# Key and value products of pairs of kv heads by Strassen's method in a fused two-layer transformer kernel

## The chip, the cores and the metric

The kernel runs on one core of one Trainium2 chip. TensorE (PE) multiplies matrices, VectorE (DVE), ScalarE (ACT) and GpSimd (POOL) do elementwise work and reductions, and SyncE (SP) issues nearly all DMA transfers in this kernel. The metric is the device time of one execution in microseconds (us). Its size is judged by the median of several runs.

## The reference

Two layers work on `x` of 4 batches x 512 rows x 512 columns, in float32. Each layer modulates `x` by an adaptive layer norm, adds a gated attention and then a gated feed-forward network (FFN). The change lies in the attention of layer 1 and at the start of the FFN after it. What is computed there:

```python
# h: modulated layer norm of x, (4, 512, 512); Hq, Hkv, D = 32, 8, 128; g = 4
q = (h @ w_q).reshape(B, S, Hkv, g, D)        # w_q 512 x 4096
k = (h @ w_k).reshape(B, S, Hkv, D)           # w_k 512 x 1024
v = (h @ w_v).reshape(B, S, Hkv, D)           # w_v 512 x 1024
scores = einsum('bqhgd,bkhd->bhgqk', q, k) * D ** -0.5
probs = softmax(where(causal, scores, -inf))
x = x + ga * (einsum('bhgqk,bkhd->bqhgd', probs, v).reshape(B, S, Hq * D) @ w_o)
h = layernorm(x) * (1 + cb) + sb
x = x + gb * down_scale * ((silu(gate(h)) * up(h)) @ down_wq.T)   # weights are integers with scales
```

## The kernel before

Layer 0 takes the first 190 us or so, the attention of layer 1 the time up to about 1778 us, and the FFN of layer 1 the rest. The attention is written out by hand, so each engine takes its instructions in the order in which the Python code emits them. The FFN is ordered by a scheduler.

**Blocks and windows.** The attention runs over 32 blocks `n`: 4 batches x 8 kv heads, each kv head with its 4 query heads. A block has two windows, `2n` (called even here) and `2n+1` (odd). A call `window(w, fill)` works on a pair of query heads: it computes scores and softmax of the next pair, heads `2w+2` and `2w+3`, in eight tiles of 128 rows (four for each head, of 512, 384, 256 and 128 columns because of the causal mask), and multiplies the probabilities of the current pair, heads `2w` and `2w+1`, by the values. It goes through slots `i`: in slot `i` it transposes tile `i-2` (`flip`, blocks of 32x32 on VectorE), normalizes tile `i-1` (`divide`, ScalarE), computes tile `i` (`score`: PE, mask and maximum on VectorE, exp on ScalarE), then in slots 6 and 8 runs `value` for one head of the current pair (PE lines `av`), and then takes its share of the list `fill`: pieces of the large products that belong to later or earlier blocks. The list is spread evenly over nine slots.

**The carry.** The transposed 32x32 blocks have to change partitions. `carry(w+1)` at the end of a window issues 16 DMA transfers of 128 KB on SyncE, from one of two buffers `prob2` (named `p` and `x` in the profile, since the second lies in the memory of `x`) to the tile `turned`, which `value` of the next window reads. There is one `turned`, so the carry starts when the last `value` of the window has read it. For the last pair of heads there is no later window: `turn` transposes its tiles on PE (lines `pT`) and ScalarE copies them into `straight`, which lies in the memory of `prob2[0]`.

**The large products.** Query (`q_pieces`) and output (`o_pieces`) products of a block are 512x512x512 and use Strassen's method in Winograd's form: seven products of quarters 256x256x256 instead of eight. A piece is one quarter product: `seven` takes a PSUM bank, issues 2x2 matmuls with 256 moving columns (lines `quarter`), and `take` adds the result to where it belongs. The weights' sums come from GpSimd (`left_sums`, `right_sums`), as do the sums of the attention output (`sums_o`); the sums of `h` are kept in `hsum` for a whole batch. Key and value products are plain: `k_pieces(n)` uses 4 matmuls of 512 columns for one head (lines `kps`), `v_pieces(n)` 16 matmuls of 128 columns (lines `vps`), each evicted by one ScalarE operation. All pieces share the three PSUM banks of `ps_sc`. The even windows take the query pieces of block `n+1` and the value pieces of block `n+1`, the odd ones the output pieces of block `n-1` and the key pieces of block `n+2`.

**Loads.** SyncE issues them in the order of the code: `load("q", n+2)` at the end of the even window and `load("o", n)` at the end of the odd one, both ahead of the carry, since `window` runs the list `late` before it; the key and value weights after the odd window. `load` has one buffer for each kind, so a load waits for the last matmul that reads the old weights.

**Around the FFN.** `small_loads` at block 23 loads scales, and the FFN's gates `gb` of the four batches, which GpSimd multiplies by the down scales. `leave_attention` puts the attention's result into `x`; for the last batch it stands at the start of the FFN, where its gates `ga` come by DMA. `first_weights` and `split_pieces` in the last block prepare the FFN's first weights and its first input, the latter on PE and ScalarE in pieces that fill the window. At the FFN's start `load(1)`, then `load(2)` and so on bring and convert the other weights.

Of the kernel before, what the change touches and what calls it, by code (L numbers as in the profile page):

```python
# [17 lines left out]
P = 128  # L18
# [15 lines left out]
def adaln_two_layers(ctx: ExitStack, tc: tile.TileContext, a, out: bass.AP):  # L34
# [5 lines left out]
    gp = ctx.enter_context(tc.tile_pool(name="gate", bufs=B))  # L40
# [8 lines left out]
    tmpp = early.enter_context(tc.tile_pool(name="tmp", bufs=2))  # L49
# [77 lines left out]
    def add_scaled(b, t, ps, gate):  # L127

        tm = tmpp.tile([P, E], F32, tag="tm", name="tm")
        nc.vector.tensor_tensor(tm, ps, gate, ALU.mult)  # L130
        nc.gpsimd.tensor_tensor(x[b][:, t, :], x[b][:, t, :], tm, ALU.add)

# [12 lines left out]
    l0x = l0.enter_context(tc.tile_pool(name="l0x", bufs=2))  # L145
    manual = tc.manual_schedule()
# [57 lines left out]
    def load(kind, n, place=None):  # L204

        g = n % HKV
        w = T["wp"].tile([P, KC, GW if kind in "qo" else D1], F32, tag=f"w{place or kind}", name=f"w{kind}1")
        if kind == "o":
            src = a["L1_attn_w_o"][g * GW : (g + 1) * GW, :]
        else:  # L210
            c = w.shape[2]
            src = a[f"L1_attn_w_{kind}"][:, g * c : (g + 1) * c]
        nc.sync.dma_start(w, src.rearrange("(k p) n -> p k n", p=P))
        weights[kind, n] = w
# [12 lines left out]
    def quarters(t):  # L227
        lo, hi = slice(0, HALF), slice(HALF, S)
        return t[:, 0:2, lo], t[:, 0:2, hi], t[:, 2:4, lo], t[:, 2:4, hi]
# [24 lines left out]
    def sums_q(n):  # L254
        s = T["wp"].tile([P, 3, 2, HALF], F32, tag="sq", name="sq")
        left["q", n] = left_sums(nc.gpsimd, weights["q", n], s)
# [25 lines left out]
    class Pieces:  # L282
# [52 lines left out]
        def wsq(self):  # L335
            sums_q(0)
# [392 lines left out]
    def seven(A, Bs, take, order):  # L729

        def piece(i):
            ps, l, r = bank([P, 2, HALF], "quarter"), A()[i], Bs()[i]
            for m in range(2):
# [27 lines left out]
    def q_pieces(n):  # L761
        u, c = {}, {}
        tt = nc.vector.tensor_tensor

        def take(i, ps):
            if i == 1:
                for j in range(2):
                    qT[n, j] = at.tile([P, 2, S], F32, tag="qT", name="qT", bufs=3)
                c[11], c[12], c[21], c[22] = corners(qT[n, 0], qT[n, 1])
                u[1] = at.tile([P, 2, HALF], F32, tag="u1", name="u1", bufs=1)  # L770
                nc.scalar.copy(u[1], ps)
            elif i == 6:
                u[2] = at.tile([P, 2, HALF], F32, tag="u2", name="u2", bufs=1)
                tt(u[2], u[1], ps, ADD)
            elif i == 2:
                tt(c[11], u[1], ps, ADD)
            elif i == 5:
                tt(u[1], u[2], ps, ADD)
            elif i == 7:
                tt(c[22], u[1], ps, ADD)  # L780
                tt(u[2], u[2], ps, ADD)
            elif i == 3:
                tt(c[12], u[1], ps, ADD)
            else:
                tt(c[21], u[2], ps, SUB)

        return seven(lambda: left["q", n], lambda: right["h", n // HKV], take, (1, 6, 2, 5, 3, 7, 4))
# [9 lines left out]

    def k_pieces(n):
        hold = {}

        def piece(i):
            if i == 0:
                hold["ps"] = bank([P, 512], "kps")
            for k in (2 * i, 2 * i + 1):
                nc.tensor.matmul(  # L805
                    hold["ps"], weights["k", n][:, k, :], h1[n // HKV][:, k, :],
                    start=(k == 0), stop=(k == KC - 1),
                )
            if i == 1:
                kT[n] = at.tile([P, S], F32, tag="kT", name="kT")  # L810
                nc.scalar.mul(kT[n], hold["ps"], float(D1) ** -0.5)  # L811

        return [lambda i=i: piece(i) for i in range(2)]

    def v_pieces(n):
        hold = {}

        def piece(i):
            if i == 0:
                hold["ps"] = bank([P, 512], "vps")  # L820
            for t in (2 * i, 2 * i + 1):
                for k in range(KC):
                    nc.tensor.matmul(  # L823
                        hold["ps"][:, t * D1 : (t + 1) * D1],
                        h1[n // HKV][:, k, t * P : (t + 1) * P], weights["v", n][:, k, :],
                        start=(k == 0), stop=(k == KC - 1),
                    )
            if i == 1:
                vs[n] = at.tile([P, NT, D1], F32, tag="v", name="v")
                nc.scalar.copy(vs[n].rearrange("p t d -> p (t d)"), hold["ps"])  # L830

        return [lambda i=i: piece(i) for i in range(2)]
# [198 lines left out]
    def small_loads():  # L1031
# [3 lines left out]
        dsb = tmpp.tile([P, E], F32, tag="tm", name="dsb")  # L1035
        nc.sync.dma_start(dsb, a["L1_ffn_down_scale"].partition_broadcast(P))
        for b in range(B):
            gb[b] = spread(1, 1, b, gp, "gb")
# [16 lines left out]
    def split_pieces(got):  # L1055

        def piece(c):
# [7 lines left out]
            tm = tmpp.tile([P, E], F32, tag="tm", name="tm")  # L1065
# [27 lines left out]
    def window(w, fill, side=(), late=()):  # L1093
# [5 lines left out]
        share = [len(fill) // 9 + (i < len(fill) % 9) for i in range(9)]  # L1099
        each = -(-len(side) // 9)  # L1100
        for i in range(10):
            if more and i > 1:
                (turn if w + 1 == LAST else flip)(*tiles[i - 2])
# [4 lines left out]
            if w >= 0 and i in (6, 8):  # L1108
# [299 lines left out]
```

## Time and profile before

| | |
|---|---|
| Median of 3 runs | 2101.63 us (2101.59 to 2102.39) |
| Profiled execution | 2105.77 us, of which its span 2104.0 |
| PE, share of the span | 98% |
| VectorE, ScalarE, GpSimd | 61%, 43%, 31% |
| Matmul rows `quarter`, `sc`, `av` in the chain | 36%, 13%, 13% |
| Matmul rows `vps`, `kps` in the chain | 5%, 5% |

The profiled execution is one run with the profiler on; it took 4.1 us more than the median. Its rows name line, engine, operation and tiles as `out<-in`; in brackets stand the idle time of the engine ahead of a row and what ended it. Busy times of PE rows overlap somewhat[...]. A block takes some 48.4 us in the steady part, from the start of one block's even window to the next.

### The profile page before, as it was taken

The numbers are of one execution on the slowest core, as the hardware profiler recorded it, in microseconds if no ns is written. First come the engines' busy times: TensorE is split into PE (matmuls) and PEld (weight loads), VectorE is DVE, ScalarE is ACT, GpSimd is POOL, SyncE is SP. The second block draws the span as 40 slices with busy tenths as digits, with TensorE's granted clock in tenths as the row PEclk, the third lists the DMA queues.
The fourth block names the chain that finished last, engine by engine and source line by source line (L and its number), as shares of the span: only waits on it lengthen the run. The fifth ranks groups of instructions, "written<-read, shape, count | busy, mean of one in ns | idle before, by whom it ended". The sixth has DMA issues, their size and how long they took to land.

```text
span 2104.0 us, 26905 instructions
## 1 busy us (share of the span) xinstructions
PE 2053.3 (98%) x9155; PEld 1558.1 (74%) x9155; DVE 1291.7 (61%) x3102; ACT 898.0 (43%) x2029; POOL 654.3 (31%) x525
## 2 busy tenths in 40 slices
PE   6999899999999999999999999999999998999998
PEld 4655677777777777777777777777777776788886
DVE  6766656666656666656676666566565665754543
ACT  3421644445444444544444454444444443332221
POOL 3314123333236222343352234335233322510010
PEclk8799999999999999999999999999999999999999
DMA  8311556665556656556665565566556545500000
GB/s 298 114 51 51 165 152 157 155 178 141 151 156 177 181 142 160 160 144 156 176 184 148 147 179 139 141 169 168 140 148 164 146 119 183 161 21 1 21 21 22
DMA packets 260516, 288.55 MB, mean 137 GB/s; under 512 B 23746, under 2 KB 200898, under 8 KB 260372
## 3 DMA queue, kind: packets, MB, share of 16 engines
q1 hardware_dynamic: 259844, 285.71, 50.1%
q8 instruction: 75, 1.23, 0.2%
q10 hardware_dynamic: 528, 1.05, 0.2%
q14 instruction: 69, 0.57, 0.1%
HBM read 142.99 MB, written 11.57 MB: 73 GB/s over the span
## 4 chain that ended last, share of the span: by engine, by line
PE 93%; DVE 2%; SPq 1%; POOL 1%; ACT 1%; DMA 1%; issue 1%; ACTq 0%; POOLq 0%; DVEq 0%
PE quarter L735 36%; PE av L914 13%; PE sc L865 13%; PE vps L823 5%; PE kps L805 5%; PE acc L1287 5%; PE p_gate L1268 4%; PE p_up L1268 4%; PE ffn L625 2%; SPq L905 1%; PE lnT L468 1%; PE modps L381 1%; PE lg L584 1%; PE qkv_ps L498 1%; PE modT_ps L394 1%
## 5 line engine op out<-in xcount | busy, mean ns | idle before, releaser
L865 PE MATMUL sc<-kT,qT 128*128 128x512 f32 (+3 forms) x1024 | 360.0, 434 | 0.7 <-ACT kT L811 0.7
L914 PE MATMUL av<-x,v 128*128 128x512 f32 x1008 | 295.3, 436 | 6.0 <-DMA wv<-in_L_attn_w_v_dram 3.7
L866 DVE TENSOR_TENSOR sc<-sc,mask 128x128 f32<-128x128 f32 x512 | 145.4, 284 | 227.3 <-PE sc L865 227.0
L914 PEld LDWEIGHTS av<-x,v 128*128 128x128 f32 x1008 | 190.2, 192 | 125.4 <-issue 80.6
L868 DVE TENSOR_REDUCE nmx<-sc 128x1 f32<-128x512 f32 (+3 forms) x512 | 251.5, 491 | 17.7
L880 ACT ACTIVATE p<-p,rden 128x512 f32<-128x512 f32 (+3 forms) x256 | 143.8, 562 | 258.9 <-DVE rden L879 258.9
L880 ACT ACTIVATE x<-x,rden 128x512 f32<-128x512 f32 (+3 forms) x256 | 143.8, 562 | 245.3 <-DVE rden L879 245.3
L865 PEld LDWEIGHTS sc<-kT,qT 128*128 128x128 f32 x1024 | 190.4, 191 | 40.0 <-issue 16.3
L794 DVE TENSOR_TENSOR acc<-acc,quarter 128x512 f32<-128x512 f32 x196 | 134.4, 687 | 132.4 <-PE quarter L735 130.5
L735 PEld LDWEIGHTS quarter<-wo,oT 128*128 128x128 f32 x768 | 146.4, 191 | 54.5 <-issue 28.7
L735 PE MATMUL quarter<-wo,oT 128*128 128x256 f32 x768 | 182.4, 381 | 2.4 <-DMA wo<-in_L_attn_w_o_dram 2.2
L235 POOL TENSOR_TENSOR sq<-wq 128x512 f32<-128x512 f32 x32 | 40.6, 1268 | 424.8 <-DMA wq<-in_L_attn_w_q_dram 418.5
L870 ACT ACTIVATE p<-sc,nmx 128x512 f32<-128x512 f32 (+3 forms) x256 | 135.0, 527 | 73.5 <-DVE nmx L868 34.0
L870 ACT ACTIVATE x<-sc,nmx 128x512 f32<-128x512 f32 (+3 forms) x256 | 134.8, 527 | 73.5 <-DMA x<-p 37.0
L235 POOL TENSOR_TENSOR soT<-oT 128x512 f32<-128x512 f32 x31 | 39.4, 1272 | 373.0 <-PE quarter L735 359.0
L883 DVE STREAM_TRANSPOSE p<-p 128x512 f32<-128x512 f32 (+3 forms) x256 | 129.6, 506 | 21.2 <-ACT p L880 19.7
L883 DVE STREAM_TRANSPOSE x<-x 128x512 f32<-128x512 f32 x248 | 125.6, 506 | 14.9 <-ACT x L880 13.1
L823 PE MATMUL vps<-wv,hT 128*128 128x128 f32 x1024 | 124.8, 275 | 0.0
L735 PE MATMUL quarter<-hsum,sq 128*128 128x256 f32 x512 | 121.0, 379 | 1.4 <-DVE hsum L248 1.4
L735 PE MATMUL quarter<-hsum,wq 128*128 128x256 f32 x512 | 121.1, 379 | 0.0
L735 PE MATMUL quarter<-so,soT 128*128 128x256 f32 x512 | 121.1, 379 | 0.0
L735 PE MATMUL quarter<-hT,wq 128*128 128x256 f32 x512 | 120.9, 379 | 0.0
(232 smaller groups left out, 3593.9 us busy)
## 6 DMA issues: line engine op xcount, KB each, us to landing
x<-p SPq DMA_DIRECT2D x512, 128.0 KB, 2.7
x<-x SPq DMA_DIRECT2D x496, 128.0 KB, 2.6
wq<-in_L_attn_w_q_dram SPq DMA_DIRECT2D x32, 1024.0 KB, 5.2
wo<-in_L_attn_w_o_dram SPq DMA_DIRECT2D x32, 1024.0 KB, 5.1
wm<-in_L_wmod_dram SPq DMA_DIRECT2D x12, 1024.0 KB, 9.8
wk<-in_L_attn_w_k_dram SPq DMA_DIRECT2D x32, 256.0 KB, 3.2
wv<-in_L_attn_w_v_dram SPq DMA_DIRECT2D x32, 256.0 KB, 3.5
xn<-x_d SPq DMA_DIRECT2D x28, 256.0 KB, 4.0
```

Of the source, the lines that this page charges most:

```text
L735: nc.tensor.matmul(ps[:, m, :], l[:, k, m * P : (m + 1) * P], r[:, k, :], start=(k == 0), stop=(k == 1),)
L794: nc.vector.tensor_tensor(osum[:, i - 1], osum[:, i - 1], ps, ADD)
L805: nc.tensor.matmul(hold["ps"], weights["k", n][:, k, :], h1[n // HKV][:, k, :], start=(k == 0), stop=(k == KC - 1),)
L823: nc.tensor.matmul(hold["ps"][:, t * D1 : (t + 1) * D1], h1[n // HKV][:, k, t * P : (t + 1) * P], weights["v", n][:, k, :], start=(k == 0) ...
L865: nc.tensor.matmul(ps[:, :w], q[:, i * P : w], kT[n][:, :w], start=True, stop=True)
L866: nc.vector.tensor_tensor(ps[:, i * P : w], ps[:, i * P : w], mask, ADD)
L868: nc.vector.tensor_reduce(nmx, ps[:, :w], AX.X, ALU.max, negate=True)
L870: nc.scalar.activation(blocks(s, i), ps[:, :w].rearrange("p (j q) -> p j q", q=BK), AF.Exp, bias=nmx, accum_out=den,)
L880: nc.scalar.mul(p, p, rden)
L883: nc.vector.transpose(blocks(s, i), blocks(s, i))
L914: nc.tensor.matmul(av.rearrange("p (a n) -> p a n", a=NG)[:, :, BK * k :], vs[n][:, k, :], pT[:, k, :, P * (s % 2) + BK * k : P * (s % 2 + ...
L1268: nc.tensor.matmul(ps[kind], w[kind][:, k, c * P : (c + 1) * P], h2[b % 2][i][:, k, :], start=(k == 0 and i == 0), stop=(k == KC - 1 and i ...
```

## The change

Key and value products are made for a pair of kv heads at once, 512x256x512 and 512x512x256, by the same seven quarter products: `k_pieces(m)` and `v_pieces(m)` for kv heads `2m` and `2m+1`. A key piece is 2 matmuls of 256 moving columns, a value piece 4 of 128. `take` becomes `gather`, shared by query, key and value; for the keys it scales too. Weights are loaded for pairs (512 KB), and GpSimd makes their sums a block ahead (`pending`). Both products now stand in even windows, the keys of the next pair where `n` is odd, the values of the current pair where `n` is even; odd windows hold output pieces alone. The first three windows are filled anew, with `value` at slots 8 and 9. In the last window of the loop `turn` follows `score` five slots later instead of two, the window has twelve slots, and the last output pieces move into it. The FFN's gates are loaded and multiplied at the start of the FFN, in its own pool, and two pools go or shrink.

```diff
 def load(kind, n, place=None):
-        g = n % HKV
-        w = T["wp"].tile([P, KC, GW if kind in "qo" else D1], F32, tag=f"w{place or kind}", name=f"w{kind}1")
+        pair = kind in "kv"
+        g = n % (HKV // 2) if pair else n % HKV
+        c = 2 * D1 if pair else GW
+        w = T["wp"].tile([P, KC, c], F32, tag=f"w{place or kind}", name=f"w{kind}1")
...
-    def sums_q(n):
-        s = T["wp"].tile([P, 3, 2, HALF], F32, tag="sq", name="sq")
-        left["q", n] = left_sums(nc.gpsimd, weights["q", n], s)
+    def sums_in(kind, n):
+        w = weights[kind, n]
+        s = T["wp"].tile([P, 3, 2, w.shape[2] // 2], F32, tag=f"s{kind}", name=f"s{kind}")
+        left[kind, n] = left_sums(nc.gpsimd, w, s)
...
         def piece(i):
-            ps, l, r = bank([P, 2, HALF], "quarter"), A()[i], Bs()[i]
-            for m in range(2):
+            l, r = still()[i], moving()[i]
+            tiles = l.shape[2] // P
+            ps = bank([P, tiles, r.shape[2]], "quarter")
+            for m in range(tiles):
...
+    def gather(start, scale=None):
+        u, c = {}, {}
+        def plus(out, v, ps, sign=1):
+            if scale is None:
+                nc.vector.tensor_tensor(out, v, ps, ADD if sign > 0 else SUB)
+            else:
+                nc.vector.scalar_tensor_tensor(out, ps, sign * scale, v, ALU.mult, ADD)
         def take(i, ps):
             if i == 1:
...
+                if scale is None:
+                    nc.scalar.copy(u[1], ps)
+                else:
+                    nc.scalar.mul(u[1], ps, scale)
             elif i == 6:
+                plus(u[2], u[1], ps)
             elif i == 2:
+                plus(c[11], u[1], ps)
             elif i == 5:
+                plus(u[1], u[2], ps)
             elif i == 7:
+                plus(c[22], u[1], ps)
+                plus(u[2], u[2], ps)
             elif i == 3:
+                plus(c[12], u[1], ps)
             else:
+                plus(c[21], u[2], ps, -1)
...
+    def k_pieces(m):
+        def start():
+            for n in (2 * m, 2 * m + 1):
+                kT[n] = at.tile([P, S], F32, tag="kT", name="kT", bufs=3)
+            return corners(*(kT[n].unsqueeze(1) for n in (2 * m, 2 * m + 1)))
+        return seven(
+            lambda: left["k", m], lambda: right["h", 2 * m // HKV],
+            gather(start, float(D1) ** -0.5), SEVENTH,
+        )
+    def v_pieces(m):
+        def start():
+            for n in (2 * m, 2 * m + 1):
+                vs[n] = at.tile([P, NT, D1], F32, tag="v", name="v")
+            v0, v1 = vs[2 * m], vs[2 * m + 1]
+            return v0[:, :2], v0[:, 2:], v1[:, :2], v1[:, 2:]
+        return seven(lambda: right["h", 2 * m // HKV], lambda: left["v", m], gather(start), SEVENTH)
...
+    def gates(pool):
+        dsb = pool.tile([P, E], F32, name="dsb")
         nc.sync.dma_start(dsb, a["L1_ffn_down_scale"].partition_broadcast(P))
         for b in range(B):
-            gb[b] = spread(1, 1, b, gp, "gb")
+            gb[b] = spread(1, 1, b, pool, f"gb{b}")
             nc.gpsimd.tensor_tensor(gb[b], gb[b], dsb, ALU.mult)
...
-            tm = tmpp.tile([P, E], F32, tag="tm", name="tm")
+            tm = at.tile([P, E], F32, tag=f"u{1 + c % 2}_{E}", name="tm", bufs=1)
...
-    def window(w, fill, side=(), late=()):
+    def window(w, fill, side=(), late=(), values=(6, 8)):
...
-        share = [len(fill) // 9 + (i < len(fill) % 9) for i in range(9)]
+        lag, turn_ = (5, turn) if w + 1 == LAST else (2, flip)
+        slots = lag + 7
+        share = [len(fill) // slots + (i < len(fill) % slots) for i in range(slots)]
...
+    sums_in("k", 0)
+    sums_in("v", 0)
     sums_wo(0)
...
-    window(-1, v_pieces(0) + k_pieces(1) + q[:1])
+    window(-1, v_pieces(0))
...
-        v = v_pieces(n + 1) if ahead else []
-        k = k_pieces(n + 2) if n + 2 < NBLK else []
+        k = k_pieces(n // 2 + 1) if n % 2 and ahead else []
+        v = v_pieces(n // 2) if n % 2 == 0 and n > 0 else []
...
-            window(0, q[1:], (), [lambda: load("q", 2)])
+            window(0, q[:5], values=(8, 9))
         elif ahead:
             late = [lambda: load("q", n + 2)] if n + 2 < NBLK else []
-            window(2 * n, q + v, side[0], late)
+            if n == 1:
+                fill = q
+            elif k:
+                fill = k[:5] + q[:5] + q[5:] + k[5:]
+            else:
+                fill = [f for i in range(3) for f in (v[2 * i], v[2 * i + 1], q[i])] + v[6:] + q[3:]
+            window(2 * n, fill, side[0], late)
         else:
             first_weights()
-            window(2 * n, o[:5] + split_pieces(got))
+            t = split_pieces(got)
+            window(2 * n, o[:2] + t[:2] + o[2:3] + t[2:] + o[3:])
...
-        if n + 2 < NBLK:
-            sums_q(n + 2)
+        if 0 < n < NBLK - 2:
+            sums_in("q", n + 2)
+        while pending:
+            sums_in(*pending.pop())
         if n == 0:
-            window(1, v + k)
+            window(1, q[5:] + k_pieces(1), (), [lambda: load("q", 2)], (8, 9))
+            sums_in("q", 2)
         else:
-            window(2 * n + 1, o + turns_ + k, side[1], [lambda: load("o", n)])
+            window(2 * n + 1, o + turns_, side[1], [lambda: load("o", n)])
         sums_o(n)
-        if n + 3 < NBLK:
-            load("k", n + 3)
-        if n + 2 < NBLK:
-            load("v", n + 2)
+        m = n // 2 + 2 if n else 2
+        if (n % 2 and n > 1 or n == 0) and 2 * m < NBLK:
+            load("k", m)
+            pending.append(("k", m))
+        if n % 2 == 0 and n > 0 and n + 2 < NBLK:
+            load("v", n // 2 + 1)
+            pending.append(("v", n // 2 + 1))
...
             load(1)
+            gates(fx)
```

## The prediction

> **What bounds the kernel now.** I read the shares by engine and the row of slices first, then busy time by stretch, then TensorE in order of time, last the waits and the queue of SyncE.
>
> ```profile
> PE 2053.3 (98%) x9155; PEld 1558.1 (74%) x9155; DVE 1291.7 (61%) x3102; ACT 898.0 (43%) x2029; POOL 654.3 (31%) x525
> ...
> PE   6999899999999999999999999999999998999998
> ...
> PE 93%; DVE 2%; SPq 1%; POOL 1%; ACT 1%; DMA 1%; issue 1%; ACTq 0%; POOLq 0%; DVEq 0%
> ```
>
> TensorE is busy 98% and is 93% of the chain that ended last. Modelled ends can hide small gaps, so I check attention by stretch: an even window, an odd window, and the last odd window, which has no K product.
>
> ```profile
> 994.56:1018.85 24.29, 24.29 (x121) 19.66 (x120) 14.61 (x39) 11.46 (x28) 8.55 (x8) 1.00 0.67 173
> 1018.85:1043.01 24.16, 24.16 (x98) 17.62 (x97) 15.68 (x41) 11.08 (x27) 6.67 (x6) 1.00 0.65 174
> 1700.59:1721.31 20.72, 20.72 (x91) 16.09 (x89) 13.96 (x37) 10.12 (x25) 1.27 (x1) 1.00 0.45 106
> ```
>
> The columns are length, then busy PE, PEld, DVE, ACT, POOL, then clock and DMA. PE fills each stretch, at full clock; the others have a third free. So PE work taken out of a window shortens it, until something else binds. The prices, from PE in order of time:
>
> ```profile
> 1017.07 1.95 PE L823 MATMUL vps<-wv,hT 128*128 128x128 f32 x16
> 1018.85 1.02 PE L865 MATMUL sc<-kT,qT 128*128 128x512 f32 x2
> 1019.72 1.89 PE L735 MATMUL quarter<-wo,oT 128*128 128x256 f32 x8
> 1021.44 0.81 PE L865 MATMUL sc<-kT,qT 128*128 128x384 f32 x2
> ...
> 1037.42 1.88 PE L805 MATMUL kps<-hT,wk 128*128 128x512 f32 x4
> 1039.13 2.32 PE L914 MATMUL av<-x,v 128*128 128x512 f32 x8
> ```
>
> Start to next start is the true price, since the ends overlap. An f32 matmul shows as two rows. One row of 128 columns costs (1018.85-1017.07)/16 = 0.111 us, of 256 columns (1021.44-1019.72)/8 = 0.215, of 512 columns (1039.13-1037.42)/4 = 0.43: the price is columns, with no fixed part to see.
>
> [...] the gating `acc<-acc,ga` takes 1138 ns beside GpSimd where `acc<-acc,quarter` with a PSUM input takes 687. The new VectorE operations have one PSUM input, so more GpSimd work shouldn't slow them. [...]
>
> **The change part by part.**
>
> 1. *K and V products.* K of a pair was 2x4 matmuls of 512 columns: 16 rows x 0.43 = 6.88 us. Now 7 quarters x 2 matmuls x 2 rows = 28 rows of 256 x 0.216 = 6.05: 0.83 less. V was 64 rows of 128 x 0.112 = 7.17; now 7x8 = 56 rows, 6.27: 0.90 less. 16 pairs x 1.73 = **27.7 us less PE work**, all on the path.
>
> Evictions: ACT had 4 of 0.59 us a pair, now 2 of half the width. VectorE gets 14 of 128x256 from PSUM a pair. No such row exists; between 128x128 (284 ns) and 128x512 (687 ns) lies 0.42 us[...]. So 2.9 us for K or for V, each in an even window of its own: 14.6+2.9 = 17.5 of some 26.9 us, hidden beside the quarters on PE. GpSimd gets 8 sums of 128x256 a pair; no such row either, so half to all of the 1.27 us of 128x512: 5 to 10 us a pair of two blocks (95 us), a block ahead of use, with the GpSimd queue idle for most of a block now (418.5 us in all for `wq`): hidden. The weights come as 16+16 loads of 512 KB for 32+32 of 256 KB, the same bytes, on SyncE behind a carry and a block ahead of use: hidden. I cost these at nothing, and likewise the split's `tm` in the tiles of `u1` and `u2`, whose writer, ACT, has ended with them by then.
>
> 2. *Windows become uneven.* K moves out of the odd windows: even ones take 24.3-3.6+6.1 = 26.8 us (V: 27.0), odd ones 24.2-3.4 = 20.7. The odd window needs 15.7 us of VectorE, 76%. The third stretch above is such a window, 20.72 us without a PE gap (without the two `sizes` reductions, 1.4 us). So I take 0 lost; bounds 0 and 0.7 a window.
>
> 3. *The carry.* At a window's end SyncE issues 16 copies of probabilities, which wait until the last `av` has read `turned`; the next `av` waits for all 16.
>
> ```profile
> 1013.13 0.38 SPq L213 DMA_DIRECT2D wq<-in_L_attn_w_q_dram  x1
> 1017.26 10.66 SPq L905 DMA_DIRECT2D x<-x  x16
> ...
> 1067.58 11.78 SPq L905 DMA_DIRECT2D x<-x  x16
> ```
>
> Issue 10.3 to 11.8 plus 2.6 to landing is 12.9 to 14.4 us from the end of `av`. The next `av` comes at slot 6: one piece, 7 score tiles (4.1) and 6 output pieces (10.4), 16.2 us (K: 15.4). Slack 1 to 3. In the even windows with V the fill now ends with the last q quarter, after that `av`, and the load of `wq` for n+2 waits for that quarter. SyncE runs in order, so the carry queued behind it starts 1.73+0.05+0.38 = 2.2 us later, with 1 MB in front of it. It lands at 15.1 to 16.6, plus 0 to 1.6 for the shared engines, against 16.2. 14 windows; 0 to 1 us each; I take **+2 in all**. After odd windows the carry starts 1.1 us late (as it did at 1722.40, `av` having ended at 1721.31), but the next `av` is over 17 us away.
>
> 4. *Start.* PE stood 0.69 for `kT`, 3.73+0.25 and 1.61+0.45 us in windows -1 to 1, the 3.73 being the first carry (landing 239.2). K's two last pieces now cover the first. In window -1 only V is left as fill, so the first carry is set by VectorE: 8 tiles x 1.35 + 7 x 0.42 = 13.7 us plus the tail, from 211 to 227, landing at 240. `av` has been put at slots 8 and 9, about 236: 4 us lost, then about 1: **-1.5** (-4 to +3).
>
> 5. *Last pair.* PE waited 3.09, 0.42, 0.33 and 2.55 us in the turns:
>
> ```profile
> 1736.97 0.55 PE L893 MATMUL pT<-ident,x 128*128 128x128 f32 x3 [3.09 <-ACT x L880]
> ...
> 1751.65 0.44 PE L893 MATMUL pT<-ident,x 128*128 128x128 f32 x2 [2.55 <-ACT x L880]
> ```
>
> ACT stood until 1735.8 because the first turned tile overwrites what the carry still reads, and all later tiles queued behind. With turns three slots later the first comes at about 1733.6, so ACT stands 1.7 us and PE has 5 us of other work that needs no freed bank. 6.4 lost becomes 1: **-5.4** (-6.4 to 0). The remaining waits (2.16 for `wo`, 0.5 for `so`) stay.
>
> 6. *FFN gates.* Five broadcasts (256 KB each) and four GpSimd products leave block 23, where they were hidden, for the FFN's start. SyncE issues them between the first and second weight loads, 5 x 0.5 us; 1.28 MB at the 280 GB/s seen there is 4.6 us, so `ga` for the last batch lands at about 1792 (old time scale) instead of 1785.6, and four gatings stand on VectorE ahead of the third hidden tile, which it reached at 1796.9; GpSimd is 5 us later with the second weights, used at 1802.5. **+1** (0 to 4).
>
> Sum: -27.7+2-1.5-5.4+1 = **-31.6 us**. The profiled execution took 2105.77 us (span 2104.0), 4.1 above the median of 2101.63. I apply the sum to the median: **2070**.
>
> **Rivals.**
> - *The short odd windows bind on VectorE or on banks.* For: 76% mean, and six slots in a row hold score and output work. Against: the 20.72 us stretch. At 0.7 us x 31: 2092.
> - *The new order starves `av`: slower.* If the 1 MB of `wq` lands (5.1 us after issue) before the carry moves, the carry lands at 2.2+5.1+13 = 20.3, 4.1 after PE wants it; 14 x 4.1 = 57: 2127. It decides from (33.6/14) 2.4 us a window. Against: wide loads run at near 400 GB/s, so 1 MB is 2.6 us, and carries issue slower than the engines take them.
> - *The work goes but PE gaps.* A K piece is 0.86 us, and three banks wait for VectorE. If each of 224 pieces leaves 0.13 us, 29 us return: 2099, no change. Against: bursts are two pieces a slot, with 0.4 us each to empty.
>
> **How the numbers follow.** My forecast, 2063 to 2078, has 0.66; better (no mid loss, start at its best) 0.06; the odd windows 0.14; no change 0.05; starved `av` 0.09. Faster 0.86, same 0.05, slower 0.09, where 0.2%, 4.2 us, is about what a measurement of this kernel can tell from no change. The range 2061 to 2092 takes in the forecast, its unknown terms and the first rival.
>
> **What would show it.** Right: no `kps` or `vps` rows, `quarter` rows up by 448 of 256 and 896 of 128 columns at unchanged prices; a pair of blocks at 95.2 us instead of 96.9; `av` not waiting for DMA; turns waiting under 2 us. Wrong: PE gaps before `av` at slot 6 of odd windows after V windows (starved), or before `sc` and `quarter` in odd windows (VectorE); prices above 0.22 and 0.115 us a row.

## The result: 2110 us instead of 2105, slightly slower

In 20 runs each, on the same chips, the changed kernel has a median of 2110.22 us (2101.1 to 2119.62) and the kernel before 2104.86 (2101.59 to 2115.7). The ratio is 1.0025, with a 95% interval of 1.0012 to 1.0037: slower by about a quarter of a per cent, at the edge of what can be measured, and 40 us from the forecast of 2070. Of these, 3.2 us lie in the base: the forecast was put on a median of three runs of the kernel before, 2101.63. The profiled execution of the changed kernel took 2109.82 us (span 2107.9), against 2105.77 before.

The page of the changed kernel: busy time by engine, the shares of the chain that ended last, the group of `av` rows (busy us, mean ns, idle us ahead of them and what ended most of it), and the copies of the carry into the second buffer (KB each, median us from issue to landing).

```profile
PE 2037.2 (97%) x9219; PEld 1582.1 (75%) x9219; DVE 1360.0 (65%) x3326; ACT 873.5 (41%) x1997; POOL 748.6 (36%) x653
...
PE 80%; DMA 7%; SPq 5%; DVE 3%; issue 2%; POOL 2%; ACT 1%; POOLq 0%; ACTq 0%; DVEq 0%
...
L917 PE MATMUL av<-x,v 128*128 128x512 f32 x1008 | 299.6, 441 | 28.9 <-DMA x<-x 13.9
...
x<-x SPq DMA_DIRECT2D x496, 128.0 KB, 2.9
```

PE is busy for 16 us less, yet the span is 4 us longer. (The 16 are less than the 27.7 of work that went. Of the 11.6 between, an estimate from the granted clock in slices of 1 us gives 5 to rows at a lower clock: busy time times the missing clock adds up to 30.2 us, before to 24.9. The rest is not assigned; the last section comes to such rows.) PE's share of the chain has fallen from 93% to 80%, and DMA with SyncE's queue has grown from 2% to 12%. The `av` rows stand idle for 28.9 us; before it was 6.0. By stretch, four windows of blocks 26 and 27 (columns as in the prediction: length, busy PE, PEld, DVE, ACT, POOL, clock, DMA share, GB/s): even with V, odd, even with K, odd.

```profile
1481.84:1508.81 26.97, 26.97 (x146) 22.35 (x145) 16.46 (x47) 12.46 (x32) 8.86 (x7) 1.00 0.49 129
1508.81:1531.40 22.59, 20.96 (x90) 16.01 (x88) 14.82 (x39) 9.57 (x24) 9.23 (x9) 1.00 0.63 150
1531.40:1558.16 26.76, 26.76 (x118) 21.42 (x117) 16.75 (x47) 12.08 (x31) 8.87 (x7) 1.00 0.59 160
1558.16:1578.88 20.72, 20.72 (x89) 16.09 (x88) 14.60 (x39) 9.54 (x24) 9.24 (x9) 1.00 0.50 125
```

Three of the four are what the prediction said, 27.0, 26.8 and 20.7 us. The odd window after V should take 20.7 too: it has 20.96 us of PE work and lasts 22.59. What ends the gap, on PE:

```profile
1504.93 2.32 PE L917 MATMUL av<-x,v 128*128 128x512 f32 x8
1507.09 1.89 PE L733 MATMUL quarter<-hsum,wq 128*128 128x256 f32 x8
1508.81 1.02 PE L868 MATMUL sc<-kT,qT 128*128 128x512 f32 x2
...
1525.06 2.40 PE L917 MATMUL av<-x,v 128*128 128x512 f32 x8 [1.63 <-DMA x<-x]
...
1534.63 1.03 PE L733 MATMUL quarter<-hT,wk 128*128 128x256 f32 x4
1535.49 1.03 PE L733 MATMUL quarter<-hsum,wk 128*128 128x256 f32 x4
```

A key piece starts 0.86 us before the next, as priced. But `av` of the odd window stands for its carry. Thirteen of the 14 odd windows after a V window whose `wq` load stands before the carry have such a wait; against 22.45 us from second `av` to second `av` without one, they lose 0.98 to 3.87 us each, 24.1 us in sum. In the fourteenth, block 22, PE had already stood 1.17 us for `size` on VectorE, as in the kernel before. SyncE and VectorE around the same window end:

```profile
1509.04 0.37 SPq L208 DMA_DIRECT2D wq<-in_L_attn_w_q_dram  x1
1509.95 12.80 SPq L908 DMA_DIRECT2D x<-x  x16
```

```profile
1506.69 0.12 DVE L882 RECIPROCAL rden<-den 128x1 f32<-128x1 f32 x1
1509.01 0.69 DVE L765 TENSOR_TENSOR qT<-u,quarter 128x512 f32<-128x512 f32 x1 [2.20 <-PE quarter L733]
1509.62 0.30 DVE L886 STREAM_TRANSPOSE x<-x 128x128 f32<-128x128 f32 x1
```

The second `av` ends at 1507.09. The first copy of the carry is issued at 1509.95, 2.86 us later, right after the last `flip` (L886). That flip's input was ready, but VectorE stood 2.20 us for the last q quarter, whose eviction (L765) is ahead of it in VectorE's order: the code of slot 8 emits `value` and then the fill piece, slot 9 the flip. The 16 copies then take 12.8 us to issue, with the 1 MB of `wq` issued 0.91 us ahead of them. Meanwhile the DMA engines are busy 97% (226 GB/s); over the carry from 1559.07 to 1569.38, issued 4.8 us behind its load, they are busy 74% (174 GB/s). Which of these matters, SyncE's wait for the load, the flip, or the 1 MB, this trace alone doesn't say.

### The profile page after: what moved, and what is told of

It is laid out like the page before. It is cut to its first block, busy times and chain, and to the rows that moved or that the text cites. A ratio compares the mean times of both kernels' runs of the same rounds, so it can differ in the third digit from the quotient of the medians.

```text
span 2107.9 us, 27434 instructions
## 1 busy us (share of the span) xinstructions
PE 2037.2 (97%) x9219; PEld 1582.1 (75%) x9219; DVE 1360.0 (65%) x3326; ACT 873.5 (41%) x1997; POOL 748.6 (36%) x653
## 3 DMA queue, kind: packets, MB, share of 16 engines
q1 hardware_dynamic: 242948, 285.71, 50.1%
## 4 chain that ended last, share of the span: by engine, by line
PE 80%; DMA 7%; SPq 5%; DVE 3%; issue 2%; POOL 2%; ACT 1%; POOLq 0%; ACTq 0%; DVEq 0%
PE quarter L733 37%; PE av L917 13%; PE sc L868 9%; PE acc L1315 5%; SPq L908 5%; PE p_up L1296 4%; PE p_gate L1296 4%; DMA x<-x 4%; DMA wq<-in_L_attn_w_q_dram 2%; PE ffn L621 2%; PE lnT L464 1%; PE modps L377 1%; PE lg L580 1%; PE qkv_ps L494 1%; PE modT_ps L390 1%
## 5 line engine op out<-in xcount | busy, mean ns | idle before, releaser
L917 PE MATMUL av<-x,v 128*128 128x512 f32 x1008 | 299.6, 441 | 28.9 <-DMA x<-x 13.9
L733 PEld LDWEIGHTS quarter<-wo,oT 128*128 128x128 f32 x768 | 146.5, 191 | 54.5 <-issue 24.1
L765 DVE TENSOR_TENSOR qT<-u,quarter 128x512 f32<-128x512 f32 x128 | 87.9, 687 | 135.9 <-PE quarter L733 135.8
L886 DVE STREAM_TRANSPOSE p<-p 128x512 f32<-128x512 f32 (+3 forms) x256 | 129.4, 506 | 20.1 <-ACT p L883 18.7
L886 DVE STREAM_TRANSPOSE x<-x 128x512 f32<-128x512 f32 x248 | 125.1, 504 | 2.1 <-ACT x L883 1.2
L765 DVE TENSOR_TENSOR u<-u,quarter 128x256 f32<-128x256 f32 (+1 forms) x144 | 85.4, 594 | 63.3 <-PE quarter L733 46.6
```

Of the source, the lines that this page charges most:

```text
L733: nc.tensor.matmul(ps[:, m, :], l[:, k, m * P : (m + 1) * P], r[:, k, :], start=(k == 0), stop=(k == 1),)
L765: nc.vector.tensor_tensor(out, v, ps, ADD if sign > 0 else SUB)
L886: nc.vector.transpose(blocks(s, i), blocks(s, i))
L917: nc.tensor.matmul(av.rearrange("p (a n) -> p a n", a=NG)[:, :, BK * k :], vs[n][:, k, :], pT[:, k, :, P * (s % 2) + BK * k : P * (s % 2 + ...
```

## The experiments

Theory A was that of the prediction's slower rival, at a smaller price: the load of `wq` waits for the last q quarter and delays the carry. Rival B was that the short odd windows bind on VectorE or on banks. Unless it says otherwise, an edit is to the changed kernel, and ratios are to the kernel before on the same chip.

### 1. The load behind the carry

```diff
-            window(2 * n, fill, side[0], late)
+            if v:
+                window(2 * n, fill, side[0], after=late)
+            else:
+                window(2 * n, fill, side[0], late)
```

`after` is a new list, which `window` runs behind the carry.

> Edit: the changed kernel, with the load of wq for n+2 issued behind the carry instead of ahead of it in the 14 even windows that make V; TensorE's order is as it was. Theory A (the load waits for the last q quarter, keeps SyncE from the carry for 2.2 us and puts 1 MB in front of it, so the next av waits): the waits of av for DMA in the odd windows after V windows, 25.6 us in sum, go; 2110 falls to about 2085 (2081 to 2090), and these odd windows take 22.4 us instead of 23.4 to 24.8. Theory B (the short odd windows bind on VectorE or on score banks, and the DMA named is not the cause): no change, 2108 to 2112, with gaps of 1 to 2 us left in the same windows, before av or before sc and quarter.

Measured: 2131.75 us, ratio 1.0112 (1.0087 to 1.0137). The time is a miss for both, yet the named windows did what A says: the odd windows after V took 22.44 to 22.45 us almost everywhere, with no DMA wait. The loss has moved on. The K windows behind them took 27.5 to 32.7 us from second `av` to second `av` instead of 25.9 or 26.4, some 47 us in sum. GpSimd and PE of this kernel at the start of one:

```profile
1547.77 1.27 POOL L230 TENSOR_TENSOR sq<-wq 128x512 f32<-128x512 f32 x1 [33.91 <-DMA wq<-in_L_attn_w_q_dram]
...
1553.04 0.72 POOL L230 TENSOR_TENSOR sk<-wk 128x256 f32<-128x256 f32 x1
1553.84 0.72 POOL L231 TENSOR_TENSOR wk<-wk 128x256 f32<-128x256 f32 x1
1554.64 0.72 POOL L232 TENSOR_TENSOR sk<-wk 128x256 f32<-128x256 f32 x1
```

```profile
1551.80 1.03 PE L733 MATMUL quarter<-hT,wk 128*128 128x256 f32 x4
1555.42 2.07 PE L733 MATMUL quarter<-hsum,sk 128*128 128x256 f32 x4 [2.59 <-POOL sk L232]
```

The sums of the key weights, ready for a block, stood on GpSimd behind those of `wq`, which now lands later. So coming late is not free for the load: it has a next reader.

### 2. The load on ScalarE's queue

```diff
-            late = [lambda: load("q", n + 2)] if n + 2 < NBLK else []
+            late = [lambda: load("q", n + 2, eng=nc.scalar if v else None)] if n + 2 < NBLK else []
```

`eng` is the engine on whose queue `load` issues its transfer.

> Edit: the changed kernel, with the same 14 loads of wq issued on ScalarE's queue at the same point, so SyncE goes straight to the carry, while the 1 MB still shares the DMA engines with it. If A holds and its two halves are each some 2.2 us a window against a slack of 1 to 3 us, the carry starts 2.2 us earlier and ends some 2 us later than alone: av waits 0 to 0.6 us, the time is 2085 to 2093. If it is the 1 MB on the engines alone that counts, nearly all of the wait stays: 2104 to 2110. If it is SyncE's standing alone, it is as with the load behind the carry, 2085. Theory B: no change, 2108 to 2112.

Measured: 2110.38 us, ratio 1.0022 (1.001 to 1.0033): no gain. SyncE's queue, VectorE and PE of this kernel, same window:

```profile
1514.81 12.45 SPq L908 DMA_DIRECT2D x<-x  x16
```

```profile
1513.84 0.69 DVE L765 TENSOR_TENSOR qT<-u,quarter 128x512 f32<-128x512 f32 x1 [2.20 <-PE quarter L733]
1514.44 0.30 DVE L886 STREAM_TRANSPOSE x<-x 128x128 f32<-128x128 f32 x1
```

```profile
1509.75 2.32 PE L917 MATMUL av<-x,v 128*128 128x512 f32 x8
1511.91 1.89 PE L733 MATMUL quarter<-hsum,wq 128*128 128x256 f32 x8
...
1529.65 2.39 PE L917 MATMUL av<-x,v 128*128 128x512 f32 x8 [1.40 <-DMA x<-x]
```

SyncE had nothing ahead of the carry, and the carry still started 2.90 us after the end of `av` (1511.91). So SyncE's wait was not what held it; the flip was: it ended at 1514.74 here. And its issue still took 12.45 us, with the 1 MB beside it on the other queue. The load went out on ScalarE's queue at 1513.88, 0.93 us ahead of the carry (0.91 in the changed kernel), and over the 14 windows the issue took 11.2 to 12.5 us, as good as with the load on SyncE's own queue (11.2 to 12.8): another queue didn't keep the two apart. The time alone says less: no gain was foreseen both for the 1 MB on the engines and for rival B.

### 3. The mirror test in the kernel before

```diff
-            window(2 * n, q + v, side[0], late)
+            window(2 * n, v + q, side[0], late)
```

> Edit: the kernel before, with v + q as the fill of its even windows instead of q + v, so that there too the last q quarter stands behind the second av and the load of wq just ahead of the carry. TensorE's work is the same. Theory A: the odd windows after the 29 even windows with such a load lose what the changed kernel's lose, 1 to 2.4 us each and 1.8 on average, since the slack to the next av is the same 16.2 us: 2105 grows by some 52 us (30 to 65), to 2157. Theory B (short odd windows are the cause; these stay 24.2 us long here, with 15.7 us of VectorE): no change, within 4 us of 2105.

Measured: 2588.97 us, ratio 1.2282 (1.2252 to 1.2312), far off. `av` waited 1.0 to 2.0 us in most odd windows, about what was foreseen, but each even window took some 15 us more; the page of this kernel names it:

```profile
L823 PE MATMUL vps<-wv,hT 128*128 128x128 f32 x1024 | 180.5, 349 | 373.4 <-DMA wv<-in_L_attn_w_v_dram 373.4
```

V at the start of the window runs into its own weight, which is issued behind the carry. A test that moves two things tells little, so the next one moves a single piece:

```diff
-            window(2 * n, q + v, side[0], late)
+            window(2 * n, q[:6] + v + q[6:], side[0], late)
```

> Edit: the kernel before, with only the last of its seven q pieces put behind the V pieces in its even windows. The earlier try with all of q behind V lost 1.1 to 1.7 us in each odd window, but 15 us in each even one, where V at the start waited for its weight; here V runs at slots 6 and 7, late enough. Theory: as the last q quarter now stands behind the second av, its eviction holds the last turn and the load of wq stands ahead of the carry: 29 odd windows lose 1.1 to 1.7 us each, 2105 grows by some 40 us (30 to 50), to 2145, with even windows at 24.2 us. If the short odd windows of the changed kernel were the cause, nothing changes here: 2103 to 2109.

Measured: 2146.89 us, ratio 1.0202 (1.0178 to 1.0225). That is 41.3 us for moving one of nine pieces behind `av`, 1.4 on average for each of 29 odd windows, which are not short here; even windows stayed at 24.28. So the loss needs no short odd window, and the short ones of experiment 1 showed no wait: together this rules out B as its cause. In the kernel before, slot 8 held half a V product, which ScalarE evicted, so nothing stood ahead of the flip on VectorE.

### 4. The load behind the carry, with its sums last

On top of experiment 1:

```diff
+        while pending:
+            sums_in(*pending.pop())
         if 0 < n < NBLK - 2:
             sums_in("q", n + 2)
-        while pending:
-            sums_in(*pending.pop())
```

> Edit: the load of wq behind the carry as in the first experiment, and GpSimd makes the sums of the K or V weights, which have been there for a block, ahead of those of wq. In the first experiment the odd windows after V windows had lost nothing, but the K windows behind them stood 2.4 us for sk, whose sums waited on GpSimd behind those of the wq that now lands some 9 us later. If that is all, the K windows are back at 25.9 us, the odd ones stay at 22.4, and the changed kernel's 2110 becomes 2085 (2081 to 2089). Rival: the sums of wq themselves come too late for the q pieces of the K windows, and part of the 46 us lost there stays: K windows above 26.5 us, 2090 to 2120.

Measured: 2084.7 us, ratio 0.99 (0.988 to 0.992), as the first theory said to within 0.3 us. SyncE and PE of this kernel:

```profile
1493.20 10.58 SPq L908 DMA_DIRECT2D x<-x  x16
1503.89 0.52 SPq L208 DMA_DIRECT2D wq<-in_L_attn_w_q_dram  x1
```

```profile
1488.14 2.32 PE L917 MATMUL av<-x,v 128*128 128x512 f32 x8
...
1506.48 2.32 PE L917 MATMUL av<-x,v 128*128 128x512 f32 x8
```

`av` ends at 1490.3 (1488.14+2.16), and the carry starts 2.9 us later, as late as in the changed kernel. But it issues in 10.58 us instead of 12.80, and `av` doesn't wait. SyncE took its transfers in order: PE was done with the old `wq` at 1492.0 (1490.30+1.72), and the load went out at 1503.89, 0.1 us after the last issue of the carry. Over all 14 such windows the issue takes 10.3 to 11.1 us, in the changed kernel 11.2 to 12.8, at the same start. The changed kernel has one window of this kind itself: window 60 makes V and has no `wq` to load; its carry starts 2.90 us after `av`, issues in 10.89, and the next `av` waits 0.04. Taking away the 1 MB alone is enough.

### 5. The second `av` behind the last piece

```diff
-            window(2 * n, fill, side[0], late)
+            window(2 * n, fill, side[0], late, (6, 9 if v else 8))
```

> Edit: the changed kernel with the second av of the V windows one slot later, so behind the last q quarter instead of ahead of it; the load of wq stays ahead of the carry on SyncE. New theory: the carry starts 2.9 us after av not because of SyncE (with the load on ScalarE's queue it started as late), but because the last turn of a score tile stands on VectorE behind the eviction of that q quarter, which comes after av. Then the carry here starts within 0.5 us of the end of av, the way to the next av is 1.7 us shorter, the 1 MB has drained for 2.2 us already: av waits 0 to 0.6 us instead of 1.8, the time is 2084 to 2094. If the start is set by SyncE and the load alone, it is the same, for the load then also goes 1.7 us ahead; what tells the two apart is where the turn ends. If neither, the carry still starts 2.5 us or more after av and av waits as before or longer: 2110 to 2130.

Measured: 2080.38 us, ratio 0.9886 (0.9864 to 0.9909), better than the 2084 to 2094 foreseen. SyncE, VectorE and PE of this kernel:

```profile
1484.32 0.37 SPq L208 DMA_DIRECT2D wq<-in_L_attn_w_q_dram  x1
1486.44 11.86 SPq L908 DMA_DIRECT2D x<-x  x16
```

```profile
1484.29 0.69 DVE L765 TENSOR_TENSOR qT<-u,quarter 128x512 f32<-128x512 f32 x1
1484.89 0.30 DVE L886 STREAM_TRANSPOSE x<-x 128x128 f32<-128x128 f32 x1
```

```profile
1484.09 2.32 PE L917 MATMUL av<-x,v 128*128 128x512 f32 x8
1500.70 2.32 PE L917 MATMUL av<-x,v 128*128 128x512 f32 x8
```

The flip ends at 1485.2, inside `av`, and the carry starts 0.2 us after `av`'s end (1486.25). The 1 MB is still ahead, but the wait is gone, although the way to the next `av` is 1.7 us shorter. So a late flip without the 1 MB fits into the slack (experiment 4), and so does the 1 MB with an early flip; together they overrun it. One reservation: the load now goes out 2.1 us ahead of the carry instead of 0.9, so the carry meets less of it (issue 10.5 to 11.9 us in the 14 windows). An early flip with the load as close as in the changed kernel was not run. A V window and the odd one after it take 47.69 us here, all PE work. With this one changed argument the kernel beats both: the median is 25 us below that of before, of the 31.6 forecast.

### 6. The last pair undone

```diff
-        lag, turn_ = (5, turn) if w + 1 == LAST else (2, flip)
+        lag, turn_ = 2, turn if w + 1 == LAST else flip
...
-            window(2 * n, o[:2] + t[:2] + o[2:3] + t[2:] + o[3:])
+            window(2 * n, o[:5] + t)
...
+            run(*o[5:])
```

> Edit: the changed kernel with the last pair as it was before: turns two slots behind their score tile instead of five, five o pieces and then the four pieces of the split in the window, the last two o pieces behind it. From the first score tile of window 62 to the first p_gate the kernel before took 57.4 us and the changed one 54.6. If the later turns are worth the 5.4 us of my sum and something else in this window took 2.6 of them back, this kernel takes some 60 us there; if they are worth 2.8 because the new order lets three more instructions stand behind the o pieces that wait for wo, it takes 57.4. In either case the whole time is 2113 to 2116, not to be told apart by itself.

Measured: 2114.24 us, ratio 1.0036 (1.0023 to 1.0049). From the first score tile of window 62 (1723.75) to `p_gate` (1780.33) it took 56.6 us, 2.0 more than the changed kernel. The waits of the changed kernel's PE there:

```profile
1729.34 3.65 PE L733 MATMUL quarter<-wo,oT 128*128 128x256 f32 x8 [2.23 <-DMA wo<-in_L_attn_w_o_dram]
...
1741.28 0.66 PE L1067 MATMUL lnT<-ident,xn 128*128 128x128 f32 x4 [0.71 <-ACT tm L1071]
1744.24 0.90 PE L896 MATMUL pT<-ident,x 128*128 128x128 f32 x3 [2.31 <-DVE acc L833]
```

The 3.09 and 2.55 us in the turns are gone; a wait of 2.31 for a bank that VectorE empties took their place. VectorE had stood 4.86 us for the first o piece, which itself waits for `wo`, and all its later work was late.

The 2.0 us are not yet the worth of the part, since the two executions ran at different clocks there. The last pair of this kernel and of experiment 2, of the kernel before and of experiment 1, and of the changed kernel (columns as above):

```profile
1723.75:1780.33 56.58, 45.03 (x199) 33.66 (x197) 22.19 (x50) 20.35 (x47) 17.55 (x17) 0.97 0.57 175
1729.52:1782.35 52.83, 44.56 (x199) 33.86 (x197) 21.82 (x50) 20.38 (x47) 17.89 (x17) 0.97 0.62 187
...
1721.31:1778.70 57.39, 46.57 (x198) 34.85 (x197) 22.69 (x50) 20.55 (x47) 17.83 (x17) 0.94 0.56 172
1748.68:1802.07 53.39, 46.02 (x199) 34.66 (x197) 22.59 (x50) 20.38 (x47) 17.69 (x17) 0.94 0.61 185
...
1726.08:1780.66 54.58, 47.18 (x198) 35.56 (x197) 21.78 (x50) 20.60 (x47) 17.98 (x17) 0.91 0.58 179
```

Experiments 1 and 2 have the changed kernel's last pair. At a clock of 0.97 and of 0.94 it is 3.7 and 4.0 us shorter than the old order; at the 1.00 of experiments 4 and 5 it took 52.1 and 51.7 us. So the part is worth about 4 us, and the changed kernel's 54.6 has slow rows in it, such as the 3.65 us above.

### 7. Three small edits, and two more

On top of experiment 4: `t[:2] + o[:3] + t[2:] + o[3:]` in the last pair; `gates` at hidden tile 11 of batch 0; `sums + [lambda: None] + ends` with one empty slot instead of three.

> A version meant to beat both: as the first of these runs (load behind the carry, K and V sums first), and three small edits: two pieces of the split ahead of the o pieces in the last pair, so that VectorE isn't held by o pieces that wait for wo (3.5 us less from the first score tile of window 62 to p_gate, 54.6 to some 51); the FFN gates made at hidden tile 11 of batch 0 instead of ahead of the second weights (1 to 1.5 us less); one empty slot instead of three ahead of the gating of acc, so that none stands in front of the last turn in blocks 9, 17 and 25 (up to 4 us less). 2085 less 6 to 9: 2077 (2072 to 2083).

Measured: 2083.04 us, ratio 0.989 (0.9869 to 0.9911): 1.7 us less than experiment 4, not 6 to 9, and within the scatter. In the trace the last pair gained 1.8 (50.3 us), which one execution can't settle: the same order took 51.6 in the last run below. The FFN gained nothing: from `p_gate` to the end it took 327.1 us, as in the changed kernel (327.2; before 325.3). Its start ran like that of before for 24 us, and then VectorE stood 1.21 us for a `rstd` that GpSimd made behind a weight for which it had stood 2.62 us. So what the gates cost is not settled. The empty slots gained less than 1 us in all: block 17 gained 1.0, the other two lost 0.3 each.

On top of experiment 5, the same order in the last pair:

> Edit: the second av of the V windows behind their last piece, as in the run that took 2080, and two pieces of the split ahead of the o pieces of the last pair. In the version with all three small edits the last pair took 50.3 us from the first score tile of window 62 to p_gate, against 52.1 in the same kernel without them; here 51.7 should fall to about 50. Whole: 2079 (2074 to 2083), which the comparison of two medians can't tell from 2080.

Measured: 2079.97 us, ratio 0.9889 (0.9869 to 0.9909). The last pair took 50.1 us in this execution, as expected. PE now waits 0.40 for `wo`, and then for its sums, with slow rows behind it (3.37 us for eight that take 1.89 elsewhere); the trace of this kernel:

```profile
1711.10 3.37 PE L733 MATMUL quarter<-so,oT 128*128 128x256 f32 x8 [3.21 <-POOL so L244]
```

And on top of that all of q in window 0:

```diff
-            window(0, q[:5], values=(8, 9))
+            window(0, q, values=(8, 9))
...
-            window(1, q[5:] + k_pieces(1), (), [lambda: load("q", 2)], (8, 9))
+            window(1, k_pieces(1), (), [lambda: load("q", 2)], (8, 9))
```

> Edit: the same, and all seven q pieces of block 1 in window 0 instead of five there and two in window 1. In the runs so far av of window 0 waits 4.8 to 5.0 us for the first carry, and its eight rows then take 4.6 us instead of 2.2, at a clock of 0.76 to 0.81 over 236 to 250 us. If the rows are slow because TensorE stood, 3.46 us of q work in front of av leaves a wait of 1.4 and rows at 2.2 to 3: av ends 1.6 to 2.4 us earlier, the second carry starts by that much earlier, and av of window 1, with 10.7 us of work ahead of it against 13, waits some 2.4. Gain: 1.5 to 3 us, 2076 (2071 to 2081). If rows are slow for another reason (what av reads), av takes 4.6 us again and ends when it did; then window 1, with 3.5 us less in it, gains nothing from it but waits for its carry: 2079.

Measured: 2079.88 us, ratio 0.9875 (0.9859 to 0.989): no gain to be seen. PE of this kernel:

```profile
238.91 3.30 PE L917 MATMUL av<-x,v 128*128 128x512 f32 x8 [2.37 <-DMA x<-p]
242.88 4.48 PE L917 MATMUL av<-x,v 128*128 128x512 f32 x8 [0.68 <-ACT oT L922]
260.09 3.99 PE L917 MATMUL av<-x,v 128*128 128x512 f32 x8 [2.37 <-DMA x<-x]
264.76 2.42 PE L917 MATMUL av<-x,v 128*128 128x512 f32 x8 [0.68 <-ACT oT L922]
```

The first wait halved, to 2.37 where 1.4 was foreseen, and a wait of 2.37 came in window 1, as planned; but now there were two waits with slow rows behind each. PE waits for the carry in both windows, so moving work between them only moves the wait.

## Why the prediction was wrong, step by step

Predicted and measured, in us of the profiled executions:

| Part | Predicted | Measured |
|---|---|---|
| 1. K and V products | -27.7 | -27.7: pieces at 0.86 and 0.90 |
| 2. Uneven windows | 0 | +6.1: 4.1 in blocks with gating, 2.0 in blocks with the next norm |
| 3. Carry after V windows | +2 | **+24.1** |
| 4. Start | -1.5 | +1.2 |
| 5. Last pair | -5.4 | -2.8 (at like clock about -4) |
| 6. FFN gates | +1 | +1.9 |

The measured column gives +2.8; the executions differ by 4.05. Of the rest 0.45 had come before the attention began and 0.5 in windows 60 and 61; some 0.3 us is not assigned.

**The step that failed is 3**, in its sizes. The prediction named the place, the load and the slack, and even gave the sign by which to see it (gaps before `av` at slot 6 of odd windows after V windows). It put the start at "2.2 us later" from SyncE alone and the cost of shared engines at "0 to 1.6", an estimate without its working. By these figures the carry lands 15.1 to 18.2 us after `av` against 16.2, so up to 2.0 us late in each of 14 windows, 28 in all; it wrote "0 to 1 us each" and took 2 in all, and gives no reason for either. The start was 2.9 us after `av`, and not by SyncE: it followed the queue of SyncE past the moved piece but not that of VectorE, where the eviction of the same piece stands ahead of the last flip. And with the 1 MB the carry's issue took 11.8 us on average in the 14 windows, where experiment 4 has 10.5. With a slack of 1 to 3 us, 0.7 us more at the start and 1.3 more in the issue were enough for 1.85 us in each of 13 windows. The step also took the average of a wait that is nil up to the slack and grows one for one beyond it: near the edge a small error in a start is the whole answer. The rival that ended slower had the right mechanism with a wrong picture, a load that lands whole before the carry moves, at 5.1 us for the load and 4.1 a window (the carry's issue grew by 1.3 us); its point of decision, 2.4 us a window, was not reached by the carry alone (24.1 in 14 windows are 1.7 each); steps 2, 4 and 5 gave the rest.

**Step 1 was right** in all it priced: four windows without waits take 95.2 us, as said (47.69 in experiment 5, and 25.91 and 21.58 for the two after it); PE rows (a matmul is two: the 32 x 16 of `vps` are 1024 rows on the page of before), evictions (128x256 took 0.41 to 0.42 us on average, 0.43 at most), sums. With GpSimd busy for 36% of the span instead of 31%, the 196 rows `acc<-acc,quarter`, with a PSUM input, took 686 ns (687 before). The 1138 ns of `acc<-acc,ga` are the mean of 16 rows of 0.68 to 1.79 us, and one of 0.69, at 669.78, stood beside GpSimd too: what sets their length isn't shown. Its "hidden" held, since the even windows with K and V had no gap in the four shown. **Step 2** was right for VectorE as an average: 14.6 us in 20.72. It overlooked that blocks 9, 17 and 25 gate `acc` late in their K windows: the flip stood behind these VectorE operations, the carry started 2.7 us late in block 9, and `av` lost 1.96, 1.21 and 0.93 us. The cause is read from the trace; the empty slots that were taken away settled it only in part. Blocks 5, 13 and 21, whose K windows also hold the norm of the next batch, lost 0.7 us each; why is open.

**Step 4** had the sign wrong. From the same q pieces (195.14 before, 195.59 now) to window 2 it takes 71.3 us instead of 69.2, of which 0.9 is more PE work, the keys of one more block, which belongs to step 1; that leaves 1.2. The wait for the first carry was 4.85 us, about the 4 foreseen, but the step compared it with waits alone; after it the eight rows of `av` took 4.60 us (before, after 3.73 us, 3.48; without a wait 2.3), and K's last pieces waited 1.07 for VectorE. **Step 5** was right about the two waits that went, and nearly about their worth, some 4 us at like clock; it missed which wait stood next: behind `wo`, on VectorE. **Step 6** was of the right size by its total, 0.7 to 2.0 us in the kernels with this FFN; which of its operations costs it is open.

## What to carry to other kernels

When a piece of work is moved, follow every engine that it touches, not only the one it was moved on: its eviction took a place in VectorE's order ahead of a small operation that a long transfer waited for. Before giving a transfer less time, add up its start, its issue and what shares the engines with it, against the slack of that very window, and leave enough of it that one of them can come late. A load that is moved out of the way has a next reader too, and on an in-order engine whatever stands behind that reader waits with it, as `sk` did on GpSimd behind the sums of `wq` in experiment 1 (PE stood 2.59 us for it).

## What the runs showed of the hardware

Rows of PE behind a wait can run at about half speed, which adds up to some 2.3 us to the eight rows of `av` (4.6 us instead of 2.3). Over 1729.30 to 1733.00 of the changed kernel, behind the wait of 2.23 us for `wo`, the granted clock was 0.54; in its windows without a wait it was 1.00. How long the wait was goes with it only at the ends. Ahead of the first `av` of windows 0 to 61, waits up to 1.92 us were followed by eight rows in 2.4 us, as good as without a wait (2.3); those of 4.78 us and more by eight rows in 4.6. In between both happened: 1.95 us gave 3.43 and 2.12 gave 2.40 (changed kernel), 2.37 gave 3.30 and 3.99 (last run of experiment 7), 3.52 gave 2.39 (experiment 3, single piece) and 3.73 gave 3.48 (kernel before). So a wait from 1.95 us on could be enough here, and one of 3.52 was not; what else decides it isn't shown.

The issue of the carry's 16 copies is no fixed time of SyncE. Over the 14 windows it took 10.3 to 11.1 us without a load near it (experiment 4), 11.2 to 12.8 with a load of 1 MB issued 0.9 us ahead, 11.2 to 12.5 with that load on ScalarE's queue (experiment 2), and 10.5 to 11.9 with it issued 2.1 us ahead (experiment 5). In 14 even windows with K of the changed kernel, where the load goes out 4.8 to 5.8 us ahead, it took 10.3 to 11.5. The kernel before shows the two apart: the load of `wq` issued at 1013.13 moved at 394 GB/s over 1015.5 to 1017.5 with the engines full (share 1.02), the carry behind it at 193 GB/s over 1018.5 to 1027.5 with a share of 0.83.
